# Fourth attention layer of a four-layer stack: one value run per unit, the denominator from a sum of the probabilities

## The chip, the cores and the metric

The kernel runs on one core of a Trainium2 chip. The metric is the device time of one execution in microseconds (us); the time before is the median of three runs. The engines are named as in the profile: PE (TensorE matmuls), PEld (its weight loads), DVE (VectorE), ACT (ScalarE), POOL (GpSimd), SP (SyncE, which issues all DMAs here). SBUF is the on-chip memory and PSUM holds matmul results, in eight banks of 128 partitions by 512 f32 words.

## The reference

Four cross-attention layers work one after the other on 8 sequences of 256 tokens by 512 features, against a context of the same size. Layers one and four have 16 heads of 32 features; the second has a single head; the third has 32 query heads on 8 key heads. A feed-forward block follows layer one. The fourth layer, which is changed, is:

```python
a = _layer_norm(audio_kv, ln_gamma, ln_beta)
Q, K, V = hidden_states @ Wq.T, a @ Wk.T, a @ Wv.T     # split into 16 heads of 32
scores = jnp.einsum('bhtd,bhsd->bhts', Q, K) * scale
attn = jax.nn.softmax(scores, axis=-1)
out = jnp.einsum('bhts,bhsd->bhtd', attn, V)
return hidden_states + jnp.tanh(gate) * (out @ Wo.T)
```

All masks admit everything. Everything is f32; projections split each operand into a rounded part and a rest and use three products of them.

## The kernel before

**Units.** A layer's attention is cut into units of one sequence and four heads (one block of 128 features): 32 units in each of layers one, three and four. Layer four's units are numbered 32 to 63 in the list that also holds layer three's 0 to 31; below, a bare unit number up to 31 is of layer three and from 32 on of layer four. A unit of layer one or four (class `Mha`) has these steps:

- `A(h)`, per head: two score matmuls (L633) into an `sm` bank, and on DVE the row maxima (L640). After the fourth head POOL splits them into two parts (L645, L646).
- `B`: PE transposes the maxima (L652, into a `pp` bank), ACT casts them to `mT` (L654), and a DMA puts them into two rows below q, so that the next matmul subtracts them.
- `C(i)`, i = 0 to 3: the scores once more, transposed: keys on partitions, chunk kt = i // 2 of 128 keys, heads 2 (i % 2) and the one after it. Two matmuls (L669) into an `st` bank, the exponential on ACT (L677) into the tile `P` of this chunk (four heads by 256 queries).
- `AV(kt)`: eight f32 matmuls with 32-column weights into the one `av` bank: for each head the values of the chunk times its probabilities into columns 0 to 255, on the head's 32 partitions, and then a block of 32 columns of ones times the same probabilities into columns 256 to 511, which gives the softmax denominator. `AV(0)` is issued in `C(2)`, `AV(1)` in `D`. They go through `Burst`, which keeps the matmuls of one call behind each other on PE; the profile records all of them at L588.
- `D`: logarithm and exponential of the negative on ACT (L700, L701) give the reciprocal of the denominator, DVE multiplies (L702), ACT and POOL split the result into the tile `at` (L705, L706), from which the out-projection works.

**Values.** `values` (L511) projects the context, and ACT copies the result from PSUM into a tile of 768 columns: for each pair of heads 32 value columns, 32 ones (a memset on POOL, L516), 32 value columns. The tile goes to DRAM (`v3d`), and `before3` loads a sequence's two chunks in one DMA (L1469) into one `V` tile.

**Order.** `pipeline` writes the program: in step t it issues `before(t+1)` and the loads of unit t+1, then `A` of unit t, `B` of unit t-1 and `C` of unit t-2 in turn, with other work (`fill`) between them by a budget, and at the end `D` of unit t-2. In layer four the fillers are the q, k and value projections of later sequences (L212, L226 with `wv`), the end of layer three, and the out-projections (L226 with `wo` and `at`, L1414). A planner then orders each engine's instructions by what it expects to be ready; `A` and `C` have a raised priority. Each engine runs its own list in order.

**Slots.** SBUF is cut by hand into slots a0 to a15 (2048 words a partition), b0 to b10 (1024), c0 to c8 (512), v0 and v1 (1536). The tables `L_SB` (layers two and three, phase `ph5`) and `L3_SB` (layer four, phase `ph6`) say which slots a tag uses in turn. A slot holds one tile; its tiles follow each other in the order in which the source asks for them, and the first instruction of the next tile waits for the last use of the one before. The three `pp` banks of PSUM (0, 1, 2) are handed out in the same way to every projection, transposition and `B`.

**The end of layer three.** A unit of layer three (class `Gqa`) ends otherwise: `D` copies its result to SBUF and sends it through DRAM (`avd`, L1273) into a tile `nd` (L1277), which uses the slots c0, c1 and c4 in turn; `E`, put 18 us of planned time later, makes the quotient (L1285 to L1287) and splits it into `at` (L1289, L1290). After the fourth unit of a sequence `l2_post` multiplies `at` with the output weights (L226, two `pp` banks), adds the residual (L1396), normalizes and stores (`h2d`, L1402); after the last sequence it also loads layer four's output weights into the same slots. `at` lies in a10 and a11 by turns, so the second sequence of layer four writes where the last of layer three was read. In the source, `l2_post` of the last sequence stands between `C` of units 34 and 35.

Of the kernel before, what the change touches and what calls it, by code (L numbers as in the profile page):

```python
# [8 lines left out]
F = mybir.dt.float32  # L9
# [3 lines left out]
ALU = mybir.AluOpType  # L13
# [5 lines left out]
P = 128  # L19
D = 512  # L20
# [28 lines left out]
def S(s):  # L49

    o = []
    for p in s.split(","):
# [7 lines left out]
             h="b9-10", xt="c0-3", bc="c4-5", m="c6-8")  # L60
A0_SB = dict(stack="a12-15", wc="a0-1", w8="a2-5", x8="a10-11", at="a6-7", stg="b3,b4,b6",
             P="b5,b0-2", V="v1,v0", vo="b7", nat="b8,b9", h="b10", hc="c0-3", xt="c4-7", bc="c8")
FA_SB = dict(fw="a8-9", pw="a2-3", gs="a4-5", ys="a10-11", stg="b3,b4,b6", hl="c0-3", hr="b7-8", xt="c0-3", x32="c4-7", bc="b9")
FF_SB = dict(fw="a12-13,a8-9", pw="a14-15,a2-3", gs="a0-1,a4-5", ys="a10-11", stg="b3,b4,v1,b1", hl="b10,b5",
             hr="b6,v0,b7,b8", xt="c0-1,c4-7", bc="c8")
L_SB = dict(wq="a12-13", wo="a0-1", ws="a8-9,a2", x8="a4-5,a3", ec="a6", pk="a7", at="a10-11", stack="a14-15",
            ks="b0,b1", P="b2,b6,b7", nat="b3,b4", h="b5,b10,b9,b8", nd="c0-1,c4", xt="c2", p1="c8",
            bc="c5-7", V="c3", va="v0", vb="v1")
L3_SB = dict(L_SB, wk="a8-9", wv="a2,a7", x8="a4-5", st5="a3", vo="b3,b4", V="v0-1",
             xt="c2", x32="c8")  # L70
ALLP = list(range(8))
PH_PS = dict(pp=[0, 1, 2], sm=[3, 4], st=[5, 6], av=[7])

# [2 lines left out]
def tile_xattn_stack(  # L76
# [31 lines left out]
    nc = tc.nc  # L108
    NTOK = x.shape[0]
    NB = NTOK // 256  # L110
# [3 lines left out]
    const = ctx.enter_context(tc.tile_pool(name="const", bufs=1))  # L114
# [5 lines left out]
    def nm(s):  # L120
        uid[0] += 1
        return f"{s}_{uid[0]}"
# [40 lines left out]
    def dram(shape, name):  # L163
        return tc.dram_tile(shape, F, name=nm(name))
# [3 lines left out]

    ident = const.tile([P, P], F, name="ident")
    make_identity(nc, ident)  # L170
    mhalf = const.tile([P, 4], F, name="mhalf")
    nc.gpsimd.memset(mhalf, -0.5)

# [10 lines left out]
    def load_w(ph, src, tag, scale=None, lo=None, stag="stg"):  # L184
        ws = []
        v = src.rearrange("(i k p) n -> i p k n", k=2, p=P)
        n = src.shape[1]
        for i in range(v.shape[0]):
            stg = ph.T([P, 2, n], F, stag)
            nc.sync.dma_start(out=stg, in_=v[i])  # L190
            w = ph.T([P, 2, 2, n], R, tag)
            split(stg, w, scale, lo)
            ws.append(w)
        return ws
# [9 lines left out]
    def sel(ws, j, kc):  # L204
        return ws[kc // 2][:, j, kc % 2, :]
# [16 lines left out]
    def tok_mm(pt, xs, tt, ws, n=D):  # L222
        k = 0
        for kc in range(4):
            for xj, wj in PASSES:
                nc.tensor.matmul(  # L226
                    pt[:, :n],
                    lhsT=sel(xs, xj, kc)[:, tt * P : (tt + 1) * P],
                    rhs=sel(ws, wj, kc),
                    start=(k == 0),  # L230
                    stop=(k == 11),
                )
                k += 1
        return 12 * n * MMUS
# [194 lines left out]
    k0d, q0d, k3d, q3d = (nat_d(n) for n in ("k0d", "q0d", "k3d", "q3d"))  # L429

    v0d = [dram([P, 2, 768], "v0d") for _ in range(NB)]
    v3d = [dram([P, 2, 768], "v3d") for _ in range(NB)]


    q2d = [[dram([2, 96, 4, 256], "q2d") for _ in range(2)] for _ in range(NB)]
# [21 lines left out]
    wk, xs0 = [], []  # L457
# [53 lines left out]
    def values(ph, xs, tts, wv, vd):  # L511
        for kt in range(2):
            pt = ph.PS("pp")
            c = tok_mm(pt, xs, tts + kt, wv)
            V = ph.T([P, 8, 3, 32], F, "vo")
            nc.gpsimd.memset(V[:, :, 1, :], 1.0)  # L516
            nc.scalar.copy(V[:, :, 0:3:2, :], pt.rearrange("p (v x d) -> p v x d", x=2, d=32))
            nc.sync.dma_start(out=vd[:, kt], in_=V.rearrange("p v x d -> p (v x d)"))
            yield c
# [34 lines left out]
    wv = load_w(ph1, wv0, "wv")  # L554
# [46 lines left out]
    class Mha:  # L601
# [56 lines left out]
        def C(self, i):  # L658
            ph, qs, ks = self.ph, self.qs, self.ks
            kt, hp = divmod(i, 2)  # L660
            if i == 0:
                self.av = ph.PS("av")
                self.ps = []
            if hp == 0:
                self.ps.append(ph.T([P, 4, 256], F, "P"))
            pt = ph.PS("st")
            for x in range(2):
                h = 2 * hp + x
                nc.tensor.matmul(  # L669
                    pt[:, x * 256 : (x + 1) * 256],  # L670
                    lhsT=ks[0:99, h, kt * P : (kt + 1) * P],
                    rhs=qs[0:99, h, :],
                    start=True,
                    stop=True,
                )
            p = self.ps[kt][:, 2 * hp : 2 * hp + 2].rearrange("p h t -> p (h t)")
            nc.scalar.activation(p, pt, AF.Exp)  # L677
            if i == 2:
                self.AV(0)


        def AV(self, kt):
            av, ft = self.av, self.ft
            with Burst() as mm:
# [3 lines left out]
                for h in (2, 3, 0, 1):  # L688
                    v = 192 * ft + 32
                    mm(av[32 * h : 32 * h + 32, 256:512], self.V[:, kt, v : v + 32], self.ps[kt][:, h], False, kt == 1)  # L690

        def D(self):
            self.AV(1)
            ph, av, ft = self.ph, self.av, self.ft
            rc = ph.T([P, 2, 256], F, "xt")
            r, o = rc[:, 0], rc[:, 1]
            if self.ph is ph2 and tanh_table[0]:
                nc.vector.reciprocal(r, av[:, 256:512])
            else:
                nc.scalar.activation(r, av[:, 256:512], AF.Ln)  # L700
                nc.scalar.activation(r, r, AF.Exp, scale=-1.0)  # L701
            nc.vector.tensor_tensor(o, av[:, 0:256], r, ALU.mult)  # L702
            hi, lo = self.at[ft // 2][:, 0, ft % 2, :], self.at[ft // 2][:, 1, ft % 2, :]
            if self.vbias is None:
                nc.scalar.copy(hi, o)  # L705
                nc.gpsimd.tensor_tensor(lo, o, fp(hi), ALU.subtract)  # L706
            else:
                bias = col(self.vbias, ft)
                nc.scalar.activation(hi, o, AF.Identity, bias=bias)
                nc.vector.scalar_tensor_tensor(lo, o, bias, fp(hi), ALU.add, ALU.subtract)  # L710
# [271 lines left out]
    free_h += S(L_SB["h"])  # L982
    ph5, ph6 = Phase(L_SB, PH_PS), Phase(L3_SB, PH_PS)
    bq25 = const.tile([P, 4], F, name="bq25")
# [4 lines left out]
    for x_ in range(2):  # L989
        nc.sync.dma_start(  # L990
            out=w2od.rearrange("(c r x) n -> x c r n", r=16, x=2)[x_],
            in_=w2o.rearrange("(c x r) n -> x c r n", x=2, r=16)[x_],
# [466 lines left out]
    def before3(t):  # L1459
        b, ft = divmod(t - n2, 4)  # L1460
        if b == 0:
            if ft == 0:
                ring3.ts = stacks(ph6, "st5", 1) + [st[0], st[1], kst[0], st[2], st[3], kst[1]]
            for t_ in ring3.ts[2 * ft : 2 * ft + 2]:
                nc.gpsimd.memset(fp(t_[96:P]), 1.0)
        if ft == 0:
            fill.until(lambda: ready[0] > NB + b and k3n[0] > b)
            V = ph6.T([P, 2, 768], F, "V")
            nc.sync.dma_start(out=V, in_=v3d[b])  # L1469
            at = Lazy(ph5)  # L1470
            for i in range(4):
                units[t + i].__dict__.update(V=V, at=at)
# [119 lines left out]
```

## Time and profile before

| what | us |
|---|---|
| median of 3 runs | 1753.07 (1752.93 to 1756.18) |
| the profiled execution, its own time | 1749.14 |
| its span, first to last instruction | 1747.4 |
| PE busy / PEld | 1616.0 / 1224.4 |
| DVE / ACT / POOL busy | 1085.8 / 864.0 / 731.1 |
| L588, all value runs of layers one, three and four, PE busy | 212.1 |

The span is split into 40 slices of 43.7 us on the page; each digit is a tenth of that slice's time in which the engine was busy. An f32 matmul appears as two records on PE and two weight loads; a matmul on rounded operands (fp32r) as one. Matmuls are pipelined, so a record is longer than the time until the next one can start; the distance between starts says what a matmul takes of PE. In the groups, the text after the bar is the idle time of the engine ahead of the instructions and what ended it. On a timeline each line is a merged row: start, length, engine, source line, operation, tile written and tiles read, and how many were merged.

### The profile page before, as it was taken

The page shows a single profiled execution, that of the slowest core. Times are in us where ns is not written, and L with a number is a line of the kernel's source. Part 1 is how long each engine was busy: PE and PEld are TensorE (multiplying, and loading weights), DVE is VectorE, ACT ScalarE, POOL GpSimd, SP SyncE. Part 2 cuts the span into 40 slices and gives each one's busy share as a digit, 9 for nine tenths or more (in the row PEclk, how much of TensorE's full clock was granted, in tenths as well). Part 3 has the DMA queues.
Part 4 walks back from the last instruction along what each step waited for, and adds up shares of the span by engine and source line. Part 5 has one row for each costly group of instructions (what it writes and reads, how often), then busy time and mean ns, then how long its engine had stood idle before and what let it go on. Part 6 is the DMA issues. An engine that isn't in the chain of part 4 may idle for free.

```text
span 1747.4 us, 28230 instructions
## 1 busy us (share of the span) xinstructions
PE 1616.0 (92%) x9984; PEld 1224.4 (70%) x9984; DVE 1085.8 (62%) x2412; ACT 864.0 (49%) x1531; POOL 731.1 (42%) x760
## 2 busy tenths in 40 slices
PE   7999999999799999999689899898878989999998
PEld 6877867777577878878456576666646767777765
DVE  6258557777757766622567577666777785655433
ACT  5336545554446566632255456454455545544444
POOL 6345145333455565531234445444436563422111
PEclk9999999999999999999789899898989999999999
DMA  8979775555632434285654575656366756776662
GB/s 294 319 240 285 220 234 190 164 153 164 188 129 88 146 119 145 77 290 218 196 175 151 190 240 174 202 177 189 97 198 180 231 164 217 213 220 210 192 182 76
DMA packets 168444, 329.16 MB, mean 188 GB/s; under 512 B 16336, under 2 KB 84336, under 8 KB 162800
## 3 DMA queue, kind: packets, MB, share of 16 engines
q1 hardware_dynamic: 168304, 327.35, 59.1%
q8 instruction: 80, 1.31, 0.3%
q14 instruction: 60, 0.49, 0.1%
HBM read 230.79 MB, written 96.49 MB: 187 GB/s over the span
## 4 chain that ended last, share of the span: by engine, by line
PE 64%; DMA 15%; DVE 9%; ACT 4%; issue 3%; POOL 3%; SPq 2%; DVEq 0%; ACTq 0%; POOLq 0%
PE pp L212 21%; PE pp L226 21%; PE av L588 8%; PE st L669 3%; PE sm L633 3%; PE st L1233 3%; PE sm L1179 2%; DMA stack<-mT 2%; DMA nat<-in_ctxT_dram 2%; DVE sm L1189 1%; DMA ws<-mnd 1%; PE pp L336 1%; PE pp L1143 1%; DMA stack<-q0d 1%; DMA nd<-avd 1%
## 5 line engine op out<-in xcount | busy, mean ns | idle before, releaser
L640 DVE TENSOR_REDUCE negm<-sm 128x2 f32<-128x512 f32 x256 | 169.8, 682 | 125.4 <-PE sm L633 124.7
L677 ACT ACTIVATE P<-st 128x512 f32<-128x512 f32 x256 | 145.7, 594 | 126.5 <-PE st L669 125.0
L212 PE MATMUL pp<-ys,fw 128*128 128x512 f32 x768 | 190.9, 398 | 6.3 <-ACT fw L178 3.8
L226 PE MATMUL pp<-pw,gs 128*128 128x512 f32 x768 | 193.3, 398 | 3.1 <-ACT gs L948 2.6
L212 PE MATMUL pp<-x,wq 128*128 128x256 f32 x1152 | 169.4, 291 | 6.9 <-ACT wq L181 3.1
L212 PEld LDWEIGHTS pp<-ys,fw 128*128 128x128 f32 x768 | 144.0, 191 | 40.4 <-ACT fw L178 4.0
L212 PEld LDWEIGHTS pp<-x,wq 128*128 128x128 f32 x1152 | 156.2, 196 | 20.5 <-issue 6.6
L226 PEld LDWEIGHTS pp<-pw,gs 128*128 128x128 f32 x768 | 142.1, 190 | 38.5 <-ACT gs L948 4.2
L588 PE MATMUL av<-P,V 128*32 128x256 f32 (+1 forms) x2188 | 164.5, 402 | 4.0 <-DVE xt L702 2.9
L1189 DVE CUSTOM_DVE_ANT_0 sm<-sm,va 128x256 f32<-128x256 f32 x256 | 104.8, 440 | 56.2 <-PE sm L1179 55.1
L1179 PE MATMUL sm<-ks,stack 96*128 96x512 f32 x256 | 111.4, 467 | 29.2 <-DMA stack<-q2d 16.3
L949 POOL TENSOR_TENSOR gs<-xt,gs 128x512 fp32r<-128x512 f32 x64 | 91.8, 1442 | 90.8 <-ACT gs L948 90.8
L1189 DVE CUSTOM_DVE_ANT_0 sm<-sm,vb 128x256 f32<-128x256 f32 x256 | 104.4, 440 | 37.8 <-PE sm L1179 36.5
L1233 PE MATMUL st<-stack,ks 100*128 100x512 f32 x256 | 103.7, 459 | 18.2 <-DMA stack<-mT 10.0
L1248 ACT ACTIVATE P<-P 128x1024 f32<-128x1024 f32 x90 | 95.1, 1059 | 50.3 <-POOL P L1244 26.0
L226 PE MATMUL pp<-wo,at 128*128 128x512 f32 x384 | 106.5, 404 | 1.3 <-ACT at L705 1.3
L944 DVE SCALAR_TENSOR_TENSOR xt<-xt,xt 128x512 f32<-128x512 f32 x64 | 66.6, 1045 | 64.5 <-ACT xt L943 64.5
L588 PEld LDWEIGHTS av<-P,V 128*32 128x32 f32 x2188 | 59.0, 109 | 57.6 <-issue 15.4
L179 POOL TENSOR_TENSOR fw<-stg,fw 128x1024 fp32r<-128x1024 f32 x32 | 81.8, 2564 | 34.7 <-ACT fw L178 19.6
L1179 PEld LDWEIGHTS sm<-ks,stack 96*128 96x128 f32 x256 | 51.5, 207 | 63.4 <-issue 30.0
L645 POOL CAST mhl<-negm 128x8 fp32r<-128x8 f32 x64 | 15.9, 249 | 187.7 <-DVE negm L640 187.7
L226 PEld LDWEIGHTS pp<-wo,at 128*128 128x128 f32 x384 | 69.8, 191 | 22.7 <-issue 3.3
(214 smaller groups left out, 3557.0 us busy)
## 6 DMA issues: line engine op xcount, KB each, us to landing
stg<-in_wfc_dram SPq DMA_DIRECT2D x32, 512.0 KB
stg<-in_wpr_dram SPq DMA_DIRECT2D x32, 512.0 KB
ws<-med SPq DMA_DIRECT2D x16, 1024.0 KB
ws<-mnd SPq DMA_DIRECT2D x16, 1024.0 KB
q2d<-nat SPq DMA_DIRECT2D x48, 256.0 KB
stack<-q2d SPq DMA_DIRECT2D x32, 384.0 KB
k0d<-nat SPq DMA_DIRECT2D x16, 512.0 KB
stack<-k0d SPq DMA_DIRECT2D x32, 256.0 KB
```

The costliest lines, as they stand in the source:

```text
L179: lo.tensor_tensor(w[:, 1], stg, fp(w[:, 0]), ALU.subtract)
L212: nc.tensor.matmul(pt[:, :n], lhsT=sel(ws, wj, kc)[:, ft * P : (ft + 1) * P], rhs=sel(xs, xj, kc), start=(k == 0), stop=(k == 11),)
L226: nc.tensor.matmul(pt[:, :n], lhsT=sel(xs, xj, kc)[:, tt * P : (tt + 1) * P], rhs=sel(ws, wj, kc), start=(k == 0), stop=(k == 11),)
L588: self.prev = nc.tensor.matmul(o, lhsT=lhsT, rhs=rhs, start=start, stop=stop, skip_group_check=True).ins
L640: nc.vector.tensor_reduce(self.negm[:, 2 * h : 2 * h + 2], pt.rearrange("p (q k) -> p q k", q=2), AX.X, ALU.max, negate=True)
L677: nc.scalar.activation(p, pt, AF.Exp)
L944: nc.vector.scalar_tensor_tensor(v, v, 1.0 / GA, u, ALU.add, ALU.mult)
L949: nc.gpsimd.tensor_tensor(lo, u, fp(hi), ALU.subtract)
L1179: nc.tensor.matmul(pts[qt], lhsT=self.qs[0:96, h, qt * P : (qt + 1) * P], rhs=self.ks[0:96].rearrange("p u k -> p (u k)"), start=True, sto ...
L1189: nc.vector.tensor_tensor_reduce(out=t, in0=t, in1=self.am[:, qt, :], scale=1.0, scalar=-3.0e38, op0=ALU.add, op1=ALU.max, accum_out=self. ...
L1233: nc.tensor.matmul(pt, lhsT=self.ks[0:100, u, kt * P : (kt + 1) * P], rhs=self.qs[0:100, 2 * hp : 2 * hp + 2, :].rearrange("p h t -> p (h ...
L1248: last["act"] = nc.scalar.activation(pf, pf, AF.Exp).ins
```

## The change

It touches layer four alone; layer one keeps the old form (`vbias` tells them apart).

- A constant tile `ones` of 32 columns is filled once at the start.
- `values` writes layer four's values as they are, 512 columns, without ones and without the memset; `v3d` shrinks accordingly, and the two chunks are loaded by two DMAs into two `V` tiles.
- `C` no longer starts a value run. It takes a third `P` tile, and after each exponential of the second chunk DVE adds the two chunks' probabilities of these two heads into it.
- `D` calls the new `AV3`: one run of twelve f32 matmuls, four heads by two chunks of values and then four times ones by the sum.
- Slots: `V` leaves v0 and v1 for c0, c1, c3 and c4 (two tiles a sequence); `P` gets v0 and v1 in addition to b2, b6 and b7 (three tiles a unit).

```diff
-L3_SB = dict(L_SB, wk="a8-9", wv="a2,a7", x8="a4-5", st5="a3", vo="b3,b4", V="v0-1",
-             xt="c2", x32="c8")
+L3_SB = dict(L_SB, wk="a8-9", wv="a2,a7", x8="a4-5", st5="a3", vo="b3,b4", V="c0-1,c3-4",
+             P="b2,b6,b7,v0,v1", xt="c2", x32="c8")
...
+    ones = const.tile([P, 32], F, name="ones")
+    nc.gpsimd.memset(ones, 1.0)
...
-    v3d = [dram([P, 2, 768], "v3d") for _ in range(NB)]
+    v3d = [dram([P, 2, D], "v3d") for _ in range(NB)]
...
             c = tok_mm(pt, xs, tts + kt, wv)
+            if vd.shape[2] == D:
+                V = ph.T([P, D], F, "vo")
+                nc.scalar.copy(V, pt)
+                nc.sync.dma_start(out=vd[:, kt], in_=V)
+                yield c
+                continue
...
             nc.scalar.activation(p, pt, AF.Exp)
-            if i == 2:
+            if self.vbias is None:
+
+                if i == 2:
+                    self.ps.append(ph.T([P, 4, 256], F, "P"))
+                if kt:
+                    o, x, y = (self.ps[j][:, 2 * hp : 2 * hp + 2] for j in (2, 0, 1))
+                    nc.vector.tensor_tensor(o, x, y, ALU.add)
+            elif i == 2:
                 self.AV(0)
...
+        def AV3(self):
+            av, ft = self.av, self.ft
+            with Burst() as mm:
+                for kt in range(2):
+                    for h in range(4):
+                        v = 128 * ft + 32 * h
+                        mm(av[32 * h : 32 * h + 32, 0:256], self.V[kt][:, v : v + 32], self.ps[kt][:, h], kt == 0, False)
+                for h in range(4):
+                    mm(av[32 * h : 32 * h + 32, 256:512], ones, self.ps[2][:, h], False, True)
+
         def D(self):
-            self.AV(1)
+            if self.vbias is None:
+                self.AV3()
+            else:
+                self.AV(1)
...
-            V = ph6.T([P, 2, 768], F, "V")
-            nc.sync.dma_start(out=V, in_=v3d[b])
+            V = [ph6.T([P, D], F, "V") for _ in range(2)]
+            for kt in range(2):
+                nc.sync.dma_start(out=V[kt], in_=v3d[b][:, kt])
```

## The prediction

> **What bounds the kernel now.** I read the page first. The 40 slices give TensorE (PE) as the engine that is always there, and the last slices hold the fourth layer:
>
> ```profile
> span 1747.4 us, 28230 instructions
> ...
> PE   7999999999799999999689899898878989999998
> ```
>
> Then the table of windows over the fourth layer's units; its value runs (all recorded at L588, the burst helper) lie between 1472 and 1740 us. Columns: window, its length, then busy us (and instructions) of PE, weight loads, VectorE, ScalarE, GpSimd, clock, DMA share, GB/s.
>
> ```profile
> 1472.00:1500.00 28.00, 27.97 (x240) 19.74 (x238) 15.31 (x31) 15.42 (x34) 12.96 (x17) 1.00 0.71 213
> 1500.00:1550.00 50.00, 50.00 (x425) 38.95 (x425) 29.04 (x50) 22.64 (x49) 15.24 (x28) 1.00 0.82 248
> ...
> 1697.00:1740.00 43.00, 39.80 (x370) 26.39 (x368) 17.54 (x30) 23.21 (x56) 6.94 (x17) 1.00 0.30 88
> sum 268.00, PE 262.51 PEld 196.66 DVE 130.29 ACT 130.95 POOL 60.92; mean PE 43.75 PEld 32.78 DVE 21.71 ACT 21.83 POOL 10.15
> ```
>
> PE is busy 262.5 of 268 us at full clock; VectorE 130.3. Until 1697 the gaps of PE are filled with projections of later batches, so PE time taken away there is time won. After 1697 some 3 of 43 us are free, and loads of q and k take part.
>
> The Trainium skill (Perfetto Trace Analysis, Identifying the Most-Contended Engine) warns that matmul occupancy is a poor measure of TensorE and wants weight-load time instead: 38.95 of 50 here. By that rule a fifth of PE would be free, and of the 22.9 us below about 17.9 would be left. The spacing below speaks against it, so my sum does not use it.
>
> **1. Runs taken off PE: -22.9 us.** The timeline, matmuls only, shows what a run costs (start, length, count):
>
> ```profile
> 1599.77 0.87 PE L212 MATMUL pp<-x,wq 128*128 128x256 f32 x6
> 1600.57 1.07 PE L588 MATMUL av<-P,V 128*32 128x256 f32 x16
> 1601.57 0.50 PE L669 MATMUL st<-ks,stack 99*128 99x256 f32 x2
> ```
> ```profile
> 1713.61 1.93 PE L588 MATMUL av<-P,V 128*32 128x256 f32 x32
> 1715.48 0.28 PE L652 MATMUL pp<-ident,mhl 128*16 128x128 f32 x1
> ```
>
> A unit's eight matmuls of one chunk make 16 records (an f32 matmul is two). From the run's first start to the next start it is 1.00 us for 16 and 1.87 us for 32: 16 more cost 0.87, so 8 more cost 0.435. Around the run comes a switch between 128-column and 32-column tiles. The six matmuls ahead start (0.87-0.28)/5 = 0.118 apart and the last at 1600.36; the run starts 0.21 after it: 0.09 lost. The pair behind takes 0.50; such a pair is 0.40 elsewhere (at 1709.84): 0.10 lost. One run of 16 therefore takes 1.19 us out of PE.
>
> Before, a unit has two: 2.38. After, one run of 24 records (8 values, 4 ones): 1.00 + 0.435 + 0.19 = 1.625. That is 0.755 a unit, times 32 units 24.2 us. In four places two runs already lie together (x32, at 1694, 1700, 1713 and 1725); there the second entry (0.32) was never paid: -1.3. Left: 22.9.
>
> **2. The add: 64 on VectorE.** None has this form (two SBUF inputs, 512 columns). Nearest: the subtraction from PSUM at L364, 0.685 us on 512 columns, and the one with both inputs in SBUF at L179, 1.21 at best on 1024. 256 columns with one PSUM input are 0.415 (L702), 512 are 0.685, so 1024 would be 1.22: two SBUF inputs cost nothing extra by themselves. I take 0.69. The dear end is the two-SBUF form at L946, 1.08 in the mean while GpSimd works. So 44 to 69 us more on VectorE: 130 becomes 174 to 199 of 268. It does not become the bound.
>
> The Trainium skill (SBUF — State Buffer, Who interferes with whom) says that a VectorE instruction with two SBUF inputs and a GpSimd instruction that reads SBUF lock each other out. The rows have it: L179 runs from 1206 to 2831 ns. GpSimd is busy 61 of 268 us here. By the rule a quarter of the adds lose part of a GpSimd instruction, an estimate of 6 us of VectorE time, beside other work.
>
> The ones wait for the second add. Queued behind them on PE are whatever the planner put next, for all units. In the middle units the run starts 1 to 6 us after the last exponential, and the ones come 0.87 us into it; the add plus one reduction ahead of it is 1.4 us: hidden. In the last eight units there is little to spare (the last exponential ends at 1736.99, the run starts 1738.33). If none is hidden: 32 x 0.69 = 22 us; if adds also free P earlier, a little below nothing. I take +2.5, 8 units by 0.3, near the hidden end. Reductions at L640 and evictions at L344 and L364 that queue behind an add are in it.
>
> **3. Values and their loads.** 16 memsets (0.31 on GpSimd) go; copies stay at 0.585; stores and loads fall by a third (768 to 512 KB a batch), eight issues more on SP at 0.35. All of it lies beside PE. The ones' memset at the start is 0.1 us beside loads. I take 0, bounds -1 and +1.
>
> **4. Slots moved: +8 us.** The values of layer four move into c0, c1, c3, c4. c0, c1 and c4 are the ring of `nd` in layer three, and each slot serves its tiles in the order of the source. `nd` of unit u lies in c(0, 1, 4)[u mod 3]: units 27 and 30 in c0, 28 and 31 in c1. The first values are asked for between D of unit 28 and D of unit 29. So c0 goes unit 27, values, unit 30; c1 goes unit 28, values, unit 31. The first two waits cost nothing (E of unit 28 ends at 1438, the values are used from 1472). But `nd` of units 30 and 31 must now wait until layer four's unit 35 has used the first values, in its only run at the end. Before:
>
> ```profile
> 1477.39 1.14 SPq L1277 DMA_DIRECT2D nd<-avd  x2
> ```
> ```profile
> 1485.99 0.42 ACT L1285 ACTIVATE nd<-nd 128x256 f32<-128x256 f32 x1 [5.02 <-DMA nd<-avd]
> ```
> ```profile
> 1479.45 1.09 PE L226 MATMUL pp<-wo,at 128*128 128x512 f32 x4
> ...
> 1488.18 1.19 PE L226 MATMUL pp<-wo,at 128*128 128x512 f32 x4
> ```
>
> `nd` of unit 30 was issued at 1454.9, of unit 31 at 1477.4, and the last out-projection of layer three (`l2_post` of batch 7, L226) ran from 1479 to 1490. It takes two of the three `pp` banks in turn, and what follows in the source on those banks waits for it: all projections of later batches. Unit 35's second run is at 1500. With nothing else to do PE would bring unit 35 forward; its `mT` was cast at 1480.7, and the eight exponentials of units 34 and 35 (0.60 each, 4.8 us together) with two runs behind them put its run at about 1493. Then 1.1 us of issue a pair and up to 7.5 us until `nd` is there (1478.5 to 1486 above), 2.7 us for E (0.42+0.42+0.73+0.40+0.73), 12 matmuls of 0.23: fillers go on at about 1506. Between 1483 and 1506 PE has units 34 to 36 (score passes 8 x 0.12 twice and a run of 1.6: 3.6 each), scores of unit 37 and half of `l2_post`, some 15 of 23 us. Lost: 8. Bounds: 0 (loads land at once, attention covers the rest) and 24 (the banks are held from 1479 to 1515, 15 of these 36 us are covered, and those 15 take 3 longer at a clock of 0.84, as in the window from 1441 to 1460).
>
> **5. The tail: +1.5 us.** From 1697 on 7 units save 5.3 us in step 1. The chain there also holds loads of q (4.7 and 4.9 us) that wait for slots. I give back 1.5; bounds 0 and 5.
>
> **Sum.** -22.9 + 2.5 + 0 + 8 + 1.5 = -10.9. On the profiled execution's 1749.14 that is 1738.2; the median shown, 1753.07, stands 3.9 above it, so 1742.
>
> **Rivals.**
> - *Nothing in the way.* If the boundary costs 0 to 2 us, 18 to 22.9 are won: 1730 to 1735. For it: 32 equal units in a full PE. Against: the order of the slots.
> - *VectorE sets the pace.* From 1500 to 1550 it would be busy 29 + 10.5 adds by 0.8 = 37 of 50 us; each late reduction holds a score bank and PE stands. At 0.1 us for each of the 128 reductions more than I count, half of the gain and more goes: 7 to 10 us, 1749 to 1752, no change. Against: PE waits on VectorE in 1.6 us of 268 now.
> - *The run falls apart.* If the planner starts it on the first chunk and waits for the last exponential and for the add, two or three short runs stand in place of one. With two, step 1 gives 32 x 0.435 = 13.9 and the sum is -1.9, 1751; with three, 32 x 0.32 = 10.2 of that goes too, +8.3, 1761. This is also the case that the change does not do what it says (one value run a unit). Against: the 1 to 6 us between the last exponential and the run.
> - *Slower: the boundary.* If `l2_post` of batch 7 holds its two banks from 1479 until 1515, the place costs the 24 us of step 4's dear end, and the sum is +5, 1758; up to 1764 if the clock falls further. It decides once the stall is above 22 us. For it: three `pp` banks, strict order. Against: mT of unit 35 is early.
>
> **Chances.** Forecast (1736 to 1748) 0.5; nothing in the way 0.2; VectorE 0.1; fallen apart 0.08; boundary 0.12. A measurement of this kernel tells about 0.2% (3.5 us) from no change. Faster by over 0.2%: 0.5 + 0.2 + 0.05 from the edge of VectorE's case = 0.75. Slower: 0.12 and three of the 0.08 = 0.15. Within: the other 0.1. The range from 1731 to 1755 leaves out the boundary's dear end, the three short runs and the lowest 1 us of the first rival: 0.17.
>
> **What would show it.** One run of 24 records a unit, 1.43 us from first start to next start; fewer would refute step 1. Adds at 0.69 in the mean. `nd` of units 30 and 31 issued just behind unit 35's run and PE idle ahead of the next L226 on `wo,at`: step 4, and without that gap the first rival is right. More than 5 us of PE waits that end on the add would speak for VectorE. I am wrong altogether if PE's order changes ahead of 1440.

## The result, and the profile after

| kernel | median, us | ratio to the kernel before, 95% interval |
|---|---|---|
| before | 1752.85 (10 runs, 1747.18 to 1756.18) | |
| changed | 1762.14 (10 runs, 1756.86 to 1768.25) | 1.0058 [1.0037, 1.0078] |

By the ratio the change makes the kernel 10 us slower (the medians are 9.3 apart). The profiled execution took 1758.87 us (span 1757.1), 9.7 more than the one of before.

The page of the changed kernel: the span and, in forty slices, how busy PE was.

```profile
span 1757.1 us, 27795 instructions
...
PE   7999989999899999999689898898979988899997
```

The table of windows that the prediction began with, for the same stretches (window, length, busy us of PE, weight loads, VectorE, ScalarE, GpSimd, then clock, DMA share, GB/s):

```profile
1472.00:1500.00 28.00, 20.39 (x156) 12.95 (x145) 16.11 (x25) 11.84 (x26) 7.32 (x12) 0.82 0.54 152
1500.00:1550.00 50.00, 45.01 (x296) 36.19 (x295) 28.95 (x51) 18.92 (x41) 19.85 (x27) 0.97 0.52 163
...
1697.00:1740.00 43.00, 39.06 (x315) 25.83 (x315) 28.67 (x49) 23.55 (x55) 9.77 (x19) 0.96 0.38 117
sum 268.00, PE 249.45 PEld 183.16 DVE 164.54 ACT 122.48 POOL 62.22; mean PE 41.58 PEld 30.53 DVE 27.42 ACT 20.41 POOL 10.37
```

PE was busy 77.97 of 78 us from 1472 to 1550; now it is busy 65.4, and at a clock of 0.82 in the first window. This is one loss. The second does not show as idle time: between 1550 and 1650 PE is busy 99.12 of 100 us, yet the sixteen units from the last exponential of unit 40 to that of unit 56 take 143.3 us, 5 less than before (148.3), where step 1 would have made it 12 less. The timeline, matmuls only, of one unit's value run and what lies in it:

```profile
1550.37 1.06 PE L596 MATMUL av<-P,V 128*32 128x256 f32 x12
1551.35 0.51 PE L677 MATMUL st<-st 99*128 99x256 f32 x2
1551.69 0.41 PE L641 MATMUL sm<-stack,ks 97*128 97x256 f32 x2
1551.94 1.56 PE L228 MATMUL pp<-wo,at 128*128 128x512 f32 x6
1553.43 0.63 PE L596 MATMUL av<-P,V 128*32 128x256 f32 x4
...
1554.88 0.62 PE L596 MATMUL av<-P,ones 128*32 128x256 f32 x4
...
1556.11 0.63 PE L596 MATMUL av<-P,ones 128*32 128x256 f32 x4
```

This should have been one line group of 24 records. It is four pieces (12, 4, 4, 4) with scores and out-projections between them. PE works through its instructions in a fixed order, so this is how the planner laid them out. In PE's list the 32 units of layer four have 76 pieces; in the list of the kernel before they have 62 (two a unit, some joined or cut). Twelve of the 32 units got the single run.

The first loss, in the lines of `nd` and of `l2_post` (SP's DMA issue, ScalarE's first step of `E`, then PE's out-projections and the first filler behind them):

```profile
1491.83 2.31 SPq L1306 DMA_DIRECT2D nd<-avd  x4
```
```profile
1497.32 0.42 ACT L1314 ACTIVATE nd<-nd 128x256 f32<-128x256 f32 x1 [1.73 <-DMA nd<-avd]
...
1501.03 0.42 ACT L1314 ACTIVATE nd<-nd 128x256 f32<-128x256 f32 x1 [2.85 <-DMA nd<-avd]
```
```profile
1499.50 1.19 PE L228 MATMUL pp<-wo,at 128*128 128x512 f32 x4 [0.86 <-POOL at L1318]
...
1509.52 2.75 PE L214 MATMUL pp<-x,wq 128*128 128x256 f32 x21 [1.17 <-DVE h L1425]
```

All four loads of `nd`, of units 30 and 31, leave together at 1491.83, right behind the start of unit 35's run at 1490.69. Before, they left at 1454.9 and 1477.4. Between the six L228 that run from 1474.16 to 1475.64 and those at 1499.50 no L228 starts, and from 1470 until 1509.52 no projection of a later sequence. The last exponentials of units 36 and 37 are 37.9 us apart (12.0 before): the mark by which this stall is recognized in every run below.

**An account of PE.** PE's list is the same in all kernels until shortly after unit 26's last value run; the last common matmul starts at 1368.49 us before and at 1364.05 in the changed kernel. From there to the start of the last matmul, I gave the time from each matmul's start to the next one's to one of four classes: value runs (up to 0.22 a wave; a wave is the matmuls that start within 0.08 us of each other on the four groups of 32 columns), switches of tile size (up to 0.1 each ahead of a piece, behind its last wave and behind the first matmul after it; a piece is an unbroken stretch of value matmuls), other matmuls (up to the median spacing of their shape), and the rest, a gap. A matmul that is slow at a lower clock adds to the gaps. The other matmuls take 254.2 to 254.8 us in every kernel; e1 to e12 number the experiments.

| | value runs | switches | gaps | sum, with the others |
|---|---|---|---|---|
| before | 62.2 | 20.9 | 36.7 | 374.1 |
| changed | 54.5 | 23.9 | 54.9 | 387.9 |
| e1, slots freed | 54.4 | 22.6 | 43.3 | 374.8 |
| e2, runs whole | 46.8 | 12.2 | 58.8 | 372.2 |
| e3, both | 48.0 | 12.8 | 42.5 | 357.5 |
| e4, both, no add | 61.8 | 12.7 | 35.0 | 364.0 |
| e5, order reversed | 51.6 | 16.8 | 40.3 | 363.2 |
| e6, adds doubled | 48.0 | 12.6 | 58.1 | 373.3 |
| e8, one slot in the way | 47.4 | 12.6 | 62.4 | 377.2 |
| e9, the change again | 54.5 | 23.9 | 58.3 | 391.4 |
| e10, e3 again | 48.0 | 12.8 | 41.5 | 356.5 |
| e11, e4 in the change's slots | 61.0 | 12.5 | 50.8 | 378.5 |
| e12, before with one run | 62.0 | 13.2 | 34.7 | 364.2 |

It rests on one trace a kernel: the same kernel twice differs by 1.0 (e3, e10) and 3.5 (changed, e9) in the sum. With waves bounded at 0.21 or 0.24, or one switch fewer, the differences between kernels move by less than 3 us.

The runs and their switches were to lose 22.9 us; the change took 4.7 off them and put 18.2 us of gaps in. The sum grows by 13.8 and the span by only 9.7, because this trace of the changed kernel reached the common matmul 4.4 us earlier; over all kernels that moment lies between 1356.3 and 1370.6 us, and no run here says how much of that is chance.

### The profile page after: what moved, and what is told of

The parts are those of the page before. It is cut to its first block, busy times and chain, and to the rows that moved or that the text cites. A ratio compares the mean times of both kernels' runs of the same rounds, so it can differ in the third digit from the quotient of the medians.

```text
span 1757.1 us, 27795 instructions
## 1 busy us (share of the span) xinstructions
PE 1615.8 (92%) x9728; PEld 1220.4 (69%) x9728; DVE 1128.3 (64%) x2476; ACT 864.2 (49%) x1531; POOL 734.7 (42%) x745
## 4 chain that ended last, share of the span: by engine, by line
PE 65%; DMA 15%; DVE 9%; ACT 3%; issue 3%; POOL 3%; SPq 2%; DVEq 0%; ACTq 0%; POOLq 0%
PE pp L214 22%; PE pp L228 20%; PE av L596 7%; PE st L677 3%; PE st L1262 3%; PE sm L641 3%; PE sm L1208 2%; DMA stack<-mT 2%; DMA ws<-mnd 1%; DVE sm L1218 1%; PE pp L1172 1%; DMA nat<-in_ctxT_dram 1%; PE pp L338 1%; PE pp L1129 1%; POOL fw L181 1%
## 5 line engine op out<-in xcount | busy, mean ns | idle before, releaser
L228 PE MATMUL pp<-pw,gs 128*128 128x512 f32 x768 | 193.5, 399 | 2.9 <-ACT gs L977 2.6
L228 PEld LDWEIGHTS pp<-pw,gs 128*128 128x128 f32 x768 | 142.1, 190 | 38.4 <-ACT gs L977 3.8
L596 PE MATMUL av<-P,V 128*32 128x256 f32 (+1 forms) x1676 | 138.5, 412 | 3.8 <-DVE xt L731 3.1
L1277 ACT ACTIVATE P<-P 128x1024 f32<-128x1024 f32 x90 | 95.1, 1058 | 50.8 <-POOL P L1273 25.4
L653 POOL CAST mhl<-negm 128x8 fp32r<-128x8 f32 x64 | 19.2, 300 | 226.7 <-DVE negm L648 226.6
L228 PE MATMUL pp<-wo,at 128*128 128x512 f32 x384 | 108.7, 406 | 2.9 <-ACT at L734 1.9
L973 DVE SCALAR_TENSOR_TENSOR xt<-xt,xt 128x512 f32<-128x512 f32 x64 | 66.7, 1046 | 63.5 <-ACT xt L972 63.5
L228 PEld LDWEIGHTS pp<-wo,at 128*128 128x128 f32 x384 | 69.5, 191 | 24.8 <-issue 4.5
L975 DVE SCALAR_TENSOR_TENSOR xt<-xt,xt 128x512 f32<-128x512 f32 x64 | 69.1, 1083 | 24.3 <-ACT xt L974 24.2
```

What stands on the lines that cost most here:

```text
L228: nc.tensor.matmul(pt[:, :n], lhsT=sel(xs, xj, kc)[:, tt * P : (tt + 1) * P], rhs=sel(ws, wj, kc), start=(k == 0), stop=(k == 11),)
L596: self.prev = nc.tensor.matmul(o, lhsT=lhsT, rhs=rhs, start=start, stop=stop, skip_group_check=True).ins
L975: nc.vector.scalar_tensor_tensor(u, v, 1.0, u, ALU.add, ALU.mult)
L1277: last["act"] = nc.scalar.activation(pf, pf, AF.Exp).ins
```

## The experiments

The theory: there are two losses, each from one detail of the change. The values' first slots hold up the end of layer three (**boundary**), and the order of matmuls within `AV3` lets the planner cut the run (**pieces**). The rivals: only one of them costs anything; or VectorE's adds are the loss. The kernels were timed in three groups (e1 to e4, e5 to e8, e9 to e12), each group on another chip and against the kernel before in the same group (medians 1754.36, 1748.25, 1749.10), so kernels of different groups are compared by their ratios; 0.001 of a ratio is 1.75 us.

### e1 to e4: each detail alone, both, and both without the add

e1, the slots:

```diff
-V="c0-1,c3-4"
+V="c3,c5,c0-1"
```

c5 held a bias row that is last read before unit 28. The first sequence's values go there and into c3; c0 and c1 serve the second sequence, behind `nd` of units 30 and 31.

> The changed kernel with one edit: the first values of layer four go into c3 and c5 (both free by then) and the second into c0 and c1, so that nd of units 30 and 31 waits for nobody. The order of the value runs stays as in the changed kernel (still cut into pieces by the planner: 71 pieces in the order of TensorE, 76 in the changed kernel, 62 before, for 32 units). Theory (two losses: the boundary, about 26 us by the milestones of the two traces, and the pieces): some 24 us less than the changed kernel, 1734 to 1742. Rival A (the pieces are the whole loss, the wait for the slots was covered): 1756 to 1762, no change against the changed kernel. Rival B (the adds on VectorE are the loss): the same, 1756 to 1762.

e2, the order in `AV3`; the slots are those of the change:

```diff
+                for h in (2, 3, 0, 1):
+                    mm(av[32 * h : 32 * h + 32, 256:512], ones, self.ps[2][:, h], True, False)
                 for kt in range(2):
-                    for h in range(4):
+                    for h in (2, 3, 0, 1):
                         v = 128 * ft + 32 * h
-                        mm(av[32 * h : 32 * h + 32, 0:256], self.V[kt][:, v : v + 32], self.ps[kt][:, h], kt == 0, False)
-                for h in range(4):
-                    mm(av[32 * h : 32 * h + 32, 256:512], ones, self.ps[2][:, h], False, True)
+                        mm(av[32 * h : 32 * h + 32, 0:256], self.V[kt][:, v : v + 32], self.ps[kt][:, h], False, kt == 1)
```

> The changed kernel with one edit: in the value run the four products with ones come first, so that its first matmul waits for the last add and nothing behind it waits for anything; the planner then leaves 33 pieces for 32 units where the changed kernel has 76. The slots stay as in the changed kernel. Theory (two losses): the pieces go, the boundary stays; units 37 to 63 took 212 us where 0.755 us a unit would have left 196, so 12 to 16 us less than the changed kernel, 1744 to 1750, and the gap of 38 us between units 36 and 37 is still there. Rival A (the pieces are the whole loss): 1734 to 1740. Rival B (the adds are the loss): 1758 to 1766, since the run now starts later than before the edit.

e3 has both edits.

> Both edits: the values in c3, c5, c0, c1 and the products with ones first (35 pieces for 32 units). Theory (two losses that add): 1762 - 24 - 14, so 1720 to 1730, below the kernel before by 1.3 to 1.9 per cent; one run of 24 records a unit at 1.43 us from first start to next start, and no gap at units 36 and 37. Rival A (one loss only, the other edit gives nothing): 1736 to 1744. Rival B (the adds): 1755 or more.

e4 is e3 without the adds and the third `P` tile, with the ones on both chunks:

```diff
-                if i == 2:
-                    self.ps.append(ph.T([P, 4, 256], F, "P"))
-                if kt:
-                    o, x, y = (self.ps[j][:, 2 * hp : 2 * hp + 2] for j in (2, 0, 1))
-                    nc.vector.tensor_tensor(o, x, y, ALU.add)
...
+                for kt in (1, 0):
+                    for h in (2, 3, 0, 1):
+                        v = 128 * ft + 32 * h
+                        mm(av[32 * h : 32 * h + 32, 0:256], self.V[kt][:, v : v + 32], self.ps[kt][:, h], kt == 1, False)
+                for kt in range(2):
+                    for h in range(4):
+                        mm(av[32 * h : 32 * h + 32, 256:512], ones, self.ps[kt][:, h], False, kt == 1)
```

> As the run before it (slots c3, c5, c0, c1), but without the adds and the third tile of probabilities: the ones are multiplied with both chunks' probabilities, in one run of 16 matmuls a unit (32 records), whose first matmul needs the last exponential (35 pieces for 32 units). Against the run with both edits it has 8 records more a unit, 0.435 us, so 13.9 us over 32 units, and no add to wait for. Theory (an add beside other work costs nearly nothing): 10 to 14 us slower than the run with both edits, 1733 to 1742, and still 0.32 us a unit better than the kernel before (1742). Rival B (the adds are the loss): faster than the run with both edits, 1725 or less while that one stays above 1750.

| run | median | ratio, 95% interval | pieces | units 36 to 37, us |
|---|---|---|---|---|
| e1, slots freed | 1747.36 | 0.9953 [0.9928, 0.9978] | 71 | 7.4 |
| e2, runs whole | 1743.28 | 0.9925 [0.9896, 0.9955] | 33 | 37.1 |
| e3, both | 1732.59 | 0.9863 [0.9827, 0.9899] | 35 | 6.2 |
| e4, both, no add | 1735.45 | 0.9896 [0.9859, 0.9932] | 35 | 10.0 |

Each edit alone turns the loss into a gain, and together they give more than either: both losses are real and nearly add (18 and 23 us alone by the ratios, 34 together; in the account 13, 16 and 30). Of the rivals, the one loss and the adds as the whole loss fall; e4, without the adds, is not the faster one. My sizes were off: e1 gave 18 where I expected 24, e2 23 where I expected 12 to 16, and e4 was 6 slower than e3 where I expected 10 to 14. The distance between two exponentials marks the stall but does not price it, since work left undone at the stall is made up later.

e1's lines at the place of the stall (SP, then PE) show the slots' side: the loads leave at the old times and the fillers go on before 1486.

```profile
1448.97 1.17 SPq L1306 DMA_DIRECT2D nd<-avd  x2
1471.93 1.13 SPq L1306 DMA_DIRECT2D nd<-avd  x2
```
```profile
1485.89 2.05 PE L214 MATMUL pp<-x,wq 128*128 128x256 f32 x15
```

e3's timeline shows the other side: one run of 24 records, first the ones, then the values, 1.43 us from first start to next start. From unit 40 to unit 56 e3 takes 137.5 us, 10.8 less than before, close to the 12 of step 1.

```profile
1558.13 0.64 PE L596 MATMUL av<-P,ones 128*32 128x256 f32 x8
1558.58 1.05 PE L596 MATMUL av<-P,V 128*32 128x256 f32 x16
1559.56 0.50 PE L641 MATMUL sm<-st 97*128 97x256 f32 x2
```

And e3's windows, against those of the changed kernel shown with the result:

```profile
1472.00:1500.00 28.00, 25.55 (x205) 19.73 (x206) 19.32 (x33) 14.55 (x32) 12.21 (x17) 1.00 0.81 216
1500.00:1550.00 50.00, 48.57 (x405) 39.40 (x405) 38.29 (x66) 24.09 (x55) 21.06 (x27) 1.00 0.79 240
```

### e5 to e8: more or fewer pieces, the add, half of the boundary

e5 has e3's slots and another order; the ones stand last again:

```diff
-                for kt in range(2):
-                    for h in range(4):
+                for kt in (1, 0):
+                    for h in (2, 3, 0, 1):
```

> As the run with both edits (slots c3, c5, c0, c1), but with another order in the run: the second chunk's values first, its last exponential's heads ahead, then the first chunk's values, then the ones at the end. The first matmul waits for the last exponential, and the ones may still wait for the second add, so the planner leaves 51 pieces for the 32 units: between the 35 with the ones first and the 71 with the order of the change. Theory (the time goes with the number of pieces): from 71 to 35 pieces it was 15.8 us, 0.44 a piece, so 16 pieces more than 35 cost 7 us: ratio to the kernel before 0.990, some 1737 to 1742. Rival (it is the start of the run, early against late, that costs): the same as with the ones first or below it, ratio 0.986, 1733; a third way (any matmul behind the add costs as in the order of the change): ratio 0.995, 1747.

e6 is e3 with a second, equal `nc.vector.tensor_tensor(o, x, y, ALU.add)` behind the first.

> As the run with both edits, with each of the 64 adds made twice (the second writes the same sum again): 64 x 0.77 us = 49 us more on VectorE, 173 becomes some 222 of 261 us, and the run's first matmul waits 0.77 us longer. Theory (adds beside other work are nearly free): up to 4 us slower than the run with both edits, 1732 to 1737. Rival (the adds cost some 8 of the 13.9 us that the eight records less should have won, since the run without adds was only 5.8 us slower): another 8 to 16 us, 1740 to 1749.

e7 is e3 with `nc.gpsimd.tensor_tensor` for the add.

> As the run with both edits, with the 64 adds on GpSimd in place of VectorE. GpSimd takes 1.35 us for 512 columns with two inputs in SBUF (the subtraction at L352), so 64 adds are 86 us and GpSimd is busy some 150 of 261 us; VectorE falls from 173 to 125. 39 pieces in the order of TensorE in place of 35. Theory (adds nearly free on either engine): within 4 us of the run with both edits. Rival 1 (the adds on VectorE held up its reductions): 4 to 8 us faster, 1725 to 1729. Rival 2 (GpSimd's queue, with the casts of at and mhl in it, becomes late): 5 to 15 us slower, 1738 to 1748.

e8 is e3 with `V="c3,c1,c0,c5"`.

> As the run with both edits, but one of the two first value tiles in c1 (slots c3, c1, c0, c5): only nd of unit 31 waits for unit 35's run, nd of unit 30 is free. 33 pieces. Theory (the last post-processing of layer three needs all four units, so one slot late is as dear as two): the stall comes back whole, ratio 0.9925 as with both slots taken, 10 to 11 us slower than the run with both edits, 1740 to 1746, and a gap of over 30 us between the exponentials of units 36 and 37. Rival (each slot costs its half): 5 us, 1735 to 1739.

| run | median | ratio, 95% interval | pieces | units 36 to 37, us |
|---|---|---|---|---|
| e5, order reversed | 1730.23 | 0.9891 [0.9857, 0.9926] | 51 | 4.1 |
| e6, adds doubled | 1735.81 | 0.9927 [0.9893, 0.9960] | 34 | 15.0 |
| e7, adds on GpSimd | 1733.95 | 0.9914 [0.9883, 0.9945] | 39 | 8.0 |
| e8, one slot in the way | 1742.60 | 0.9971 [0.9949, 0.9994] | 33 | 33.7 |

- e5: with the slots freed, 71, 51 and 35 pieces stand at 0.9953, 0.9891 and 0.9863, in order as the theory has it. The two ends are apart; e5's interval stops just short of e1's and overlaps e3's, so the times alone do not exclude the rival 0.986. The account is clearer: runs and switches take 77.0, 68.4 and 60.8 us, 0.43 to 0.48 us for each piece more.
- e6: another 64 adds cost 11 us, with 9 of uncertainty. That speaks for the rival and against "up to 4", which lies just inside the interval. PE's waits in e6 put only 0.6 us down to the add itself; what grows is what comes behind it (what waited, for what, us in total, times, longest). The execution traced is 9 us above e6's median, so the list shows where the time goes and not how much:

```profile
PE st L677 <- DMA stack<-mT: 4.9, 5, 1.6
PE st L677 <- DMA ks<-mT: 4.0, 3, 2.5
PE av L596 <- DVE xt L732: 2.5, 3, 1.3
PE sm L641 <- DVE negm L648: 2.1, 3, 1.1
```

  The row maxima, from which `mT` is made, and the multiplication that empties the one `av` bank stand in VectorE's list with the adds. In e3 the two `mT` lines are 2.7 us together, and neither of the other two is among its waits. That the adds make these waits is argued from the lists, not shown by a run of its own.
- e7: not faster than e3, and by the ratios 9 us slower, but the intervals overlap: undecided between no change and the late queue. The add takes 1288 ns there.
- e8: one slot brings back the whole stall, 19 us (with 7 of uncertainty), where two late slots cost 11 to 19, and not half. In its lines unit 30's load is early and unit 31's late, and that is enough, because `l2_post` needs all four units of the sequence:

```profile
1449.74 1.14 SPq L1306 DMA_DIRECT2D nd<-avd  x2
1495.91 1.21 SPq L1306 DMA_DIRECT2D nd<-avd  x2
```
```profile
1481.41 2.27 PE L228 MATMUL pp<-wo,at 128*128 128x512 f32 x9
1504.69 2.07 PE L228 MATMUL pp<-wo,at 128*128 128x512 f32 x4
```

### e9 to e12: the ends side by side, the boundary without adds, the merging alone

e9 is the changed kernel as it stands, e10 is e3.

> The changed kernel as it stands, once more, so that it stands beside the next run on one chip. By its first measurement: ratio to the kernel before 1.004 to 1.008.

> The kernel with both edits once more (slots c3, c5, c0, c1; products with ones first), beside the changed kernel on one chip. By its first measurement: ratio to the kernel before 0.983 to 0.990. Theory (boundary and pieces are the whole of the loss): 1.9 per cent, 34 us, below the changed kernel; rival (part of that was the chip): less than 1.2 per cent below it.

e11 is e4 with the change's `V="c0-1,c3-4"`.

> The run without adds (ones multiplied with both chunks' probabilities, 16 matmuls in one run a unit), but with the values in the slots of the change (c0, c1, c3, c4): the boundary alone, on a base that has no add and no pieces (34). Theory: the run without adds stood at 0.9896 of the kernel before; the boundary adds 11 us (with the ones first) to 18 us (with the order of the change): 0.996 to 1.000, and the gap of over 30 us between units 36 and 37 is there. Rival (the stall is made by the adds and the slots together): 0.990 to 0.992.

e12 starts from the kernel before:

```diff
-            if i == 2:
+            if i == 2 and self.vbias is not None:
                 self.AV(0)
...
+        def AV2(self):
+            av, ft = self.av, self.ft
+            with Burst() as mm:
+                for kt in (1, 0):
+                    for h in (2, 3, 0, 1):
+                        v = 192 * ft + 96 * (h // 2) + 64 * (h % 2)
+                        mm(av[32 * h : 32 * h + 32, 0:256], self.V[:, kt, v : v + 32], self.ps[kt][:, h], kt == 1, False)
+                for kt in (1, 0):
+                    for h in (2, 3, 0, 1):
+                        v = 192 * ft + 32
+                        mm(av[32 * h : 32 * h + 32, 256:512], self.V[:, kt, v : v + 32], self.ps[kt][:, h], False, kt == 0)
...
-            self.AV(1)
+            if self.vbias is None:
+                self.AV2()
+            else:
+                self.AV(1)
```

> The kernel before with one edit: the first chunk's values and ones are no longer multiplied when its probabilities are there, but in one run with the second chunk's at the end of the unit (16 matmuls, 32 records; 36 pieces in place of 62). Columns of ones, slots and loads stay as they were before the change, and there is no add. Theory (a run apart costs 0.32 us of TensorE, whatever is in it): 32 - 4 - 2 runs saved by 0.32, so 8 to 10 us less than before, ratio 0.994 to 0.996. Rival 1 (the run without adds, at 0.9896, owes its gain to the merging alone): 0.988 to 0.991. Rival 2 (the three slots for probabilities hold each unit's first chunk longer, and the next unit's exponentials wait): 1.000 or more.

| run | median | ratio, 95% interval | pieces | units 36 to 37, us |
|---|---|---|---|---|
| e9, the change again | 1760.19 | 1.0063 [1.0039, 1.0088] | 76 | 40.3 |
| e10, both edits again | 1722.68 | 0.9852 [0.9827, 0.9876] | 35 | 6.1 |
| e11, e4 in the change's slots | 1750.34 | 1.0005 [0.9988, 1.0022] | 34 | 35.3 |
| e12, before with one run | 1739.54 | 0.9946 [0.9927, 0.9965] | 36 | 12.2 |

- e9 and e10 repeat the ends side by side: the two edits are worth 2.1 per cent, 37 us. The changed kernel with both is 1.5 per cent faster than the kernel before, the best version here.
- e11: the boundary without adds and pieces costs 19 us. So it comes to 18 (the change to e1), 11 (e2 to e3), 19 (e3 to e8) and 19 (e4 to e11), each difference with 6 to 8 us of uncertainty; in the account the gaps differ by 11.6, 16.3, 19.9 and 15.8. The rival, that slots and adds make the stall together, falls.
- e12: merging the two runs, and nothing else, gains 9 us, as 26 runs at 0.32 have it (8.3); in the account, runs and switches fall by 7.9.

e12 to e4 is another 9 us (0.9946 to 0.9896; intervals touch). What lies between them is the plain values without columns of ones, the smaller loads, and five slots for `P` in place of three. Which of these it is was not tried, and it may be chance: the two were timed on different chips, and in the account, from the common matmul on, they are equal (364.2 and 364.0).

## Why the prediction was wrong, point by point

The forecast was 1742 us, 11 below; it came out 10 above.

**Step 1 failed: "One run of 24".** The sizes in it were right. e3, where the run is whole, has 1.43 us as predicted, and its account is 22.3 us less for runs and switches than before, against 22.9. (The Trainium skill, Perfetto Trace Analysis, Identifying the Most-Contended Engine, judges TensorE's headroom by the useful share of its peak FLOPs and by the weight-load time; the estimate made from the weight-load time alone was 17.9, and the spacing of the starts was the better guide here.) But the change does not make one run. The rival *the run falls apart* had the mechanism and got a chance of 0.08, because "the 1 to 6 us between the last exponential and the run" seemed to speak against it. That was the wrong thing to look at. That run, `AV(1)`, started with heads 2 and 3 of the second chunk, whose exponential is the unit's last; once its first matmul could go, all could. `AV3` starts with head 0 of the first chunk, ready three exponentials earlier, and ends with ones that need an add. `Burst` only keeps a matmul behind its predecessor and gives it priority; it cannot hold other work back while the next one waits. The first matmul was early and the rest were not, so the planner filled the holes; with the matmuls that are ready last put first (e2), 76 pieces become 33. The trace of before even had the pattern and its price, in the few units that it had cut:

```profile
1490.49 1.07 PE L588 MATMUL av<-P,V 128*32 128x256 f32 x16
1491.49 0.50 PE L669 MATMUL st<-stack,ks 99*128 99x256 f32 x2
1491.92 0.62 PE L588 MATMUL av<-P,V 128*32 128x256 f32 x4
1492.48 0.50 PE L633 MATMUL sm<-stack 97*128 97x256 f32 x2
1492.91 1.06 PE L588 MATMUL av<-P,V 128*32 128x256 f32 x12
```

From first start to next start the piece of 4 takes 0.56 us and the piece of 12 takes 0.98; as one run of 16 they take 1.00. My rival priced a piece at 0.32, from two pieces that were both full. In the changed kernel the 76 pieces take, by size:

| records | 4 | 8 | 12 | 16 | 20 | 24 |
|---|---|---|---|---|---|---|
| pieces | 29 | 23 | 5 | 5 | 2 | 12 |
| us, first start to next start | 0.556 | 0.569 | 0.988 | 1.001 | 1.420 | 1.433 |

That is 59.2 us by these usual values, where 32 whole runs are 45.9; with 44 more switches outside this time, at 0.09 (ahead alone) to 0.19 (ahead and behind), it is 17 to 22 us more, and of the 22.9 between 1 and 6 are left (the account says 4.7). By the account a piece more costs 0.43 us (78.4 less 60.8 for 41 pieces), not 0.32. That the rival's case of three runs a unit stands at 1761, next to the measured 1762, is therefore chance: there were 2.4 pieces a unit, each dearer than priced, and the boundary probably cost more than its 8. (The rival's two-run case also leaves out the 1.3 that step 1 takes off.)

**Step 2, the adds at +2.5: too small, as far as is known.** An add takes 0.683 us in the median, as predicted, but 0.78 in the mean: a few are much longer (see the last section). The adds' row among VectorE's groups in the changed kernel from 1472 on (count, then busy us and mean ns, then idle time ahead):

```profile
L692 DVE TENSOR_TENSOR P<-P,P 128x512 f32<-128x512 f32 x60 | 45.8, 784 | 7.6 <-ACT P L685 6.4 <-ACT mT L662 1.2
```

e4 has eight records more a unit than e3, 13.9 us, and was only 6 slower: so some 8 us went to the adds and the third tile, and the account has 7.5 us more gaps in e3 than in e4. Doubling the adds cost 11. Each of these times has about 9 us of uncertainty, so the size stays open; they point to 0.1 to 0.2 us an add, although the add itself is never long on PE's list of waits. *VectorE sets the pace* had named the way (late maxima) and seems to be a part of the cause, the smallest.

**Step 3, values at nothing:** not tried alone; see e12 to e4.

**Step 4, the boundary at +8: the mechanism as told, the size probably too small.** The loads leave just behind unit 35's run (1491.8; I had 1493), PE stands before the next L228 and fillers go on at 1509.5 (I had 1506). The cost is 11 to 19 us, within the bounds of 0 and 24. I had counted 15 of 23 us as covered, but the account has 11.6 us (the change to e1) to 19.9 (e3 to e8) more gaps; these hold the slower clock too (0.66 from 1480 to 1490, 0.83 from 1490 to 1510). The rival *slower: the boundary* needed more than 22 us to make the kernel slower alone by more than the noise (18.9 to turn the sign), and alone it does not: e2 has the whole stall and is faster than before.

**Step 5, the tail at +1.5: too small.** From unit 56's last exponential to the end it is 54.2 us before, 52.8 in e3 and 53.2 in e10: 1.0 to 1.4 of the 5.3 are gained, so some 4 are given back, within 0 to 5. (The 5.3 should have been 4.3: three of the four places with joined runs, whose second entry the prediction took off in step 1, lie in the tail.)

**Together.** With whole runs and free slots the forecast would have been -22.9 + 2.5 + 1.5 = -18.9; e3 and e10 are 24 and 26 us below the kernel before (intervals 18 to 30), and 16.6 and 17.6 below it in the account, which holds only what comes behind the common matmul. Where the other 7 to 8 us lie, ahead of that matmul, in the one trace of before or in the noise, no run tells. (The first rival's 18 to 22.9 left the adds and the tail out; with them it is 17 to 19.) What the change as written adds to that is the pieces, 16 to 23 us by the ratios (e1 to e3; the change to e2), and the boundary.

**The last sign.** "I am wrong altogether if PE's order changes ahead of 1440": it does, some 70 us ahead. Behind the common matmul the first projections of a later sequence stand one matmul earlier in the changed kernel (first before, then changed):

```profile
1368.49 0.62 PE L1233 MATMUL st<-stack,ks 100*128 100x512 f32 x2
1368.96 1.11 PE L212 MATMUL pp<-x,wq 128*128 128x256 f32 x8
```
```profile
1364.05 0.39 PE L1262 MATMUL st<-stack,ks 100*128 100x512 f32 x1
1364.28 0.63 PE L214 MATMUL pp<-x,wq 128*128 128x256 f32 x4
```

So a change in layer four's code reached back into layer three's end. By itself it is not the loss: e1 to e11 all part from the list of before at this matmul, and e3 and e10 are among the fastest.

## What to carry to other kernels

In a run that must stay together under a planner, let the first instruction be the one that is ready last; look at what each instruction of the new run waits for, not only at when the old run started. When tiles move into slots that another phase still uses, write down the order of each slot's tiles by the source: one late tile among four is as dear as all, and here the remedy was another slot out of those that were already free. And price a short piece by its own row: half-filled ones cost as much as full ones.

## What the runs showed of the hardware that I had not expected

- **Two matmuls cost as much as four.** With 32-column tiles, pieces of 4 and 8 records take 0.556 and 0.569 us, 12 and 16 take 0.988 and 1.001, 20 and 24 take 1.420 and 1.433: here time goes by rounds of four matmuls on four column groups, some 0.43 us each and 0.13 for the piece, and a round that is begun is paid whole.
- **Single runs at half the pace.** In one run of the changed kernel the waves, which start 0.22 us apart elsewhere, start 0.43 apart, and the run takes 2.54 us in place of 1.43:

```profile
1716.96 1.94 PE L596 MATMUL av<-P,V 128*32 128x256 f32 x16
1718.67 0.90 PE L596 MATMUL av<-P,ones 128*32 128x256 f32 x8
1719.51 0.28 PE L660 MATMUL pp<-ident,mhl 128*16 128x128 f32 x1
```

  The window of 10 us around it has a granted clock of 0.83 with PE busy 8.01:

```profile
1710.00:1720.00 10.00, 8.01 (x73) 4.89 (x72) 5.75 (x10) 3.84 (x11) 1.86 (x4) 0.83 0.55 176
```

  e2 and e3 have such a run too, at 1705.99 (2.72) and 1695.74 (2.66), in windows of 10 us with a clock of 0.83; the six windows of before have 1.00 throughout. In these windows the lower clock comes only where PE has gaps, but not wherever it has them: in e2's first window PE is busy 20.09 of 28 us at 1.00.

```profile
1472.00:1500.00 28.00, 20.09 (x188) 13.30 (x180) 17.15 (x29) 13.72 (x30) 7.87 (x12) 1.00 0.64 182
```

  So some of what is won can go to the clock; when it does, these runs do not tell.
- **Some GpSimd casts wait beside the adds.** The median cast of `mhl` (L645, after L653) in layer four is as long as before (191 and 190 ns), but 7 of 32 take more than 230 ns, up to 652, and each of the 7 overlaps an add; before it is one, of 379. Single adds reach 1687 ns where the median is 683. Without adds (e4, e11) no cast is longer than 194 ns, and with the adds on GpSimd itself (e7) none longer than 198. This agrees with the lock between two-input VectorE and GpSimd instructions that the prediction took from the Trainium skill (SBUF — State Buffer, Who interferes with whom).
